# Keeping back the side matmuls of every odd slot of a scan pipeline

## The chip, the core and the metric

The kernel runs on one NeuronCore of a Trainium2 chip. The metric is the device time of one execution in microseconds; the median of the runs shown is 17,875.02 us. The core's engines are named as in the profile: PE (TensorE matmul) and PEld (its weight loads), DVE (VectorE), ACT (ScalarE), POOL (GpSimd), and SP (the queue that issues the DMAs). Each of them executes its own instructions in the order in which the program issues them; between engines they wait for each other through semaphores.

## The reference

Eight images of 48 x 48 x 96 go through four residual layers, `x = x + f(norm(x))`, all in float32:

- layer 0 and layer 3 are 2-D selective scans: an input projection to 192 channels and a 3 x 3 depthwise convolution, then a scan with 16 states per channel over four directions (rows and columns, each forward and backward), then a layer norm, a gate and an output projection;
- layer 1 upsamples by two in the frequency domain, applies a two-layer network with a quadratic in between, filters and downsamples;
- layer 2 scans each row and each column by itself, forward and backward, with a short causal convolution, a gate and an output projection.

The heart of layers 0, 2 and 3 is the same recurrence, with one state for each of 192 channels x 16:

```python
dA = jnp.exp(dl[..., None] * A)
h = h * dA + (dl * u)[..., None] * Bv[:, :, None, :]
y = jnp.einsum('bkdn,bkn->bkd', h, Cv)
```

## The kernel before

**Three stages.** `ss2d("l0", ...)` computes layer 0, `lines(...)` layer 2, and `ss2d("l3", ...)` layer 3. Layer 1 has no stage of its own. It is a *guest* (`class Guest`): a generator of small pieces, each a few matmuls into one PSUM bank and an ACT operation that reads the bank. The guest's pieces are slipped into layers 0 and 2.

**Blocks, turns and slots.** In each stage `scans` walks over 160 blocks (8 images x 4 directions x 5 blocks of up to 480 pixels). A block has four *turns* (`q` = 0 to 3), so a stage has 640 turns and the kernel 1,920. A turn handles two of a block's eight *slots*, `at = 2 * t` and `at + 1`, so slot 2q is even and slot 2q + 1 is odd. On the engines, one turn consists of:

- DVE: three scans (`scan(t, 0..2)`, L304) and those products `dbu` (L272) that are not on POOL. The scans read the decay factors from PSUM, where there are two buffers `ps_da`.
- ACT: three pairs of exponentials that fill those buffers (`make_da`, L296). The first pair of the next turn, `make_da(t + 1, 0)`, is issued after the first side step of this turn. ACT also copies rows to PSUM (`copy_b`, L253).
- POOL: two products with C (`make_hc`, L310), one for each half-turn, and its share of the `dbu` products (L272).
- PE: two *sums over states*, `reduce(t - 1, 0)` and `reduce(t - 1, 1)` (L330 and L332), each four matmuls on quarters of the array. They belong to the turn before and each needs one `make_hc`. Where a new half block begins (`slot == 0` in `reduce`, which falls into the turns with odd `q`) an *opening* matmul (L326) is issued ahead of the first sum. There is one PSUM bank `ps_y`: the opening waits until the finished sum of the half block before has been copied out (`ysum`, ACT L716, in `ss2d`; `gated`, DVE L876, in `lines`).

**Side work.** After the second sum comes `aside(at)`, and at the end of the turn `aside(at + 1)`. A side step settles the guest piece of the slot before (its ACT operation), issues the loads of the slot, takes one step of `side` (convolution, norm, output of an image), runs the steps that `stage1` has planned for this slot, and lets the guest issue its next pieces. Most of it is written so that a matmul is issued in one slot and its reader, on ACT or DVE, in the next one or two. In `ss2d`, for example, the step of slot 3 issues a matmul `raw(0)` (L665), slot 4 reads it (`biased(0)`, ACT L669) and issues `raw(1)`, slot 5 reads that, and slot 6 takes a softplus (L693). In `lines`, slot 3 is half of the convolution (L813), slot 7 two `dt` matmuls (L841) that need ACT's copy `bcl` (L835) of the same slot, and slot 9 (slot 1 of the next block) the two gate matmuls (L854), which ACT reads in slot 10 (`zb`, L863); the projection (L885) follows in that slot and is added by DVE a slot later (L893, L891). Guest pieces are read by ACT at L1073, L1102, L1109, L1119, L1125 and L1165. In layer 0 a guest piece can be issued in slots 2 to 6; in `lines` in slots 0, 2, 3 and 6.

The order of one turn is written out by hand:

```python
            if t > 0:
                reduce(t - 1, 0)
            scan(t, 1)
            make_da(t, 2)
            copy_b(at + 3)
            make_dbu(at + 3, nc.vector)
            if t > 0:
                reduce(t - 1, 1)
            aside(at)
            begin(t + 2)
            make_hc(t, 0)
            make_da(t + 1, 0)
            scan(t, 2)
            copy_b(at + 4)
            finish(at + 1)
            aside(at + 1)
```

On PE the queue therefore reads, turn after turn: first sum, second sum, matmuls of the even slot, matmuls of the odd slot.

## Time and profile before

| what | value |
|---|---|
| runs shown | 17,866.05 / 17,875.02 / 17,882.01 us |
| profiled execution | 17,892.97 us, span 17,891.2 us, mean granted PE clock 0.777 |
| busy, whole span | PE 82%, DVE 89%, ACT 78%, POOL 85% |
| stage `l0`, its 640 turns | from 115 to 5,965 us |
| stage `lines` | from 6,061 to 12,310 us |
| stage `l3` | from 12,434 to 17,857 us |

The busy shares are averages over three stages that differ in their side work, so a stage has to be read by itself. PE's busy time is modelled from pipelined matmuls, so a busy PE is not a PE at its peak. "PEclk" in the profile is the granted share of PE's full clock. A wait is listed as the idle time of an engine before an instruction, with the instruction that ended it.

### The profile page before, as it was taken

How to read it: one execution, taken by the hardware profiler on the slowest of the kernel's cores; microseconds unless marked ns; L12 is line 12 of the kernel's file. 1: busy time of each engine (PE TensorE's matmuls, PEld its weight loads, DVE VectorE, ACT ScalarE, POOL GpSimd, SP SyncE). 2: the span in 40 equal slices, each digit the busy share in tenths (PEclk: the TensorE clock that was granted, in tenths of full speed). 3: DMA queues.
4: the chain of work that ended last, by engine and by line, in shares of the span. 5: the costliest groups of instructions: out<-in, count | busy, mean ns of one | idle time of the engine just before them, and what ended most of it. 6: DMA issues, size and time to landing. Idle time of an engine off the chain costs nothing. (4 is left out here: it accounts for less than half of the span.)

```text
span 17891.2 us, 168509 instructions
## 1 busy us (share of the span) xinstructions
PE 14657.1 (82%) x53740; PEld 4413.6 (25%) x53740; DVE 15977.6 (89%) x9976; ACT 13880.5 (78%) x20932; POOL 15155.4 (85%) x7999
## 2 busy tenths in 40 slices
PE   6878888878787788888888888987778778778776
PEld 1223232323232322222222222222122222222221
DVE  7998999898888788787888889996999999999998
ACT  6877878878787677787777778786878778778776
POOL 7988888888888677787777778886999999999998
PEclk7778777878786788888888888888677777777776
DMA  4555545454545334443443444443455455455454
GB/s 141 176 166 171 172 165 170 162 178 159 168 159 174 131 137 153 137 150 133 152 144 140 144 146 156 154 154 124 170 173 173 169 174 176 168 176 177 169 175 142
DMA packets 887917, 2843.63 MB, mean 159 GB/s; under 512 B 353468, under 2 KB 421788, under 8 KB 760206
## 3 DMA queue, kind: packets, MB, share of 16 engines
q1 hardware_dynamic: 887022, 2832.85, 46.7%
q8 instruction: 421, 6.90, 0.2%
q14 instruction: 474, 3.88, 0.1%
HBM read 2384.40 MB, written 448.17 MB: 158 GB/s over the span
## 5 line engine op out<-in xcount | busy, mean ns | idle before, releaser
L304 DVE TENSOR_TENSOR_SCAN dbu<-ps_da,dbu 128x968 f32<-128x968 f32 (+3 forms) x5760 | 11823.5, 2074 | 923.6 <-ACT ps_da L296 757.6
L310 POOL TENSOR_TENSOR dbu<-dbu,bc 128x1440 f32<-128x1440 f32 (+1 forms) x3840 | 10071.8, 2635 | 2349.7 <-DVE dbu L304 2264.9
L296 ACT ACTIVATE ps_da<-dd,w_l_a 128x484 f32<-128x484 f32 (+3 forms) x11520 | 7424.3, 649 | 2511.4 <-DVE dbu L304 2282.1
L330 PE MATMUL ps_y<-dbu,w_red 128*32 128x480 f32 (+1 forms) x23040 | 4741.8, 731 | 1238.5 <-POOL dbu L310 1225.2
L332 PE MATMUL ps_y<-dbu,w_red 128*32 128x480 f32 (+1 forms) x7680 | 4705.9, 731 | 0.0
L272 DVE TENSOR_TENSOR dbu<-dd,ps_b 128x962 f32<-128x962 f32 (+5 forms) x2880 | 3828.8, 1329 | 270.3 <-ACT ps_b L253 160.7
L272 POOL TENSOR_TENSOR dbu<-dd,bc 128x481 f32<-128x481 f32 (+5 forms) x2240 | 3914.8, 1763 | 23.3 <-DMA dd<-dd 18.9
L330 PEld LDWEIGHTS ps_y<-dbu,w_red 128*32 128x32 f32 x23040 | 797.7, 126 | 5072.2 <-POOL dbu L310 2976.6
L253 ACT COPY ps_b<-bc 128x482 f32<-128x482 f32 (+3 forms) x2720 | 1448.3, 532 | 209.9 <-DVE dbu L272 164.4
L536 PE MATMUL ps_side<-xpad,w_l_cw 128*128 128x480 f32 (+1 forms) x2880 | 1466.0, 651 | 42.1 <-ACT g_room L1109 12.7
L296 ACT ACT_TABLE_LOAD x993 | 1274.0, 1283 | 17.4
L665 PE MATMUL ps_s<-bcl,dtw 6*96 6x480 f32 (+1 forms) x1280 | 952.0, 835 | 290.6 <-ACT dds L669 133.5
L813 PE MATMUL ps_sb<-xpad,w_l_cw 128*128 128x480 f32 (+1 forms) x1280 | 879.0, 839 | 90.4 <-ACT g_room L1109 33.7
L326 PE MATMUL ps_y<-ysum,w_ident 96*96 96x480 f32 (+1 forms) x960 | 764.5, 887 | 207.5 <-ACT ysum L716 203.3
L470 POOL TENSOR_TENSOR dds<-dds,u 96x960 f32<-96x960 f32 (+1 forms) x320 | 706.8, 2209 | 209.7 <-ACT dds L693 209.3
L675 PE MATMUL ps_s<-u,w_l_xp 96*38 96x480 f32 (+1 forms) x1280 | 837.5, 785 | 53.1 <-ACT g_room L1109 13.6
L813 PE MATMUL ps_sa<-xpad,w_l_cw 128*128 128x480 f32 (+1 forms) x1280 | 864.6, 826 | 0.1
L536 PEld LDWEIGHTS ps_side<-xpad,w_l_cw 128*128 128x128 f32 x2880 | 579.0, 216 | 890.5 <-issue 784.3
L332 PEld LDWEIGHTS ps_y<-dbu,w_red 128*32 128x32 f32 x7680 | 730.8, 126 | 0.0
L716 ACT COPY ysum<-ps_y 96x480 f32<-96x480 f32 (+1 forms) x640 | 472.0, 738 | 62.9 <-PE ps_y L332 61.5
L830 PE MATMUL ps_sa<-ub,w_l_xp 96*38 96x480 f32 (+1 forms) x640 | 344.3, 669 | 205.1 <-ACT ub L820 205.1
L669 ACT ACTIVATE dds<-ps_s,w_l_dtb 96x480 f32<-96x480 f32 (+1 forms) x640 | 405.5, 634 | 132.8 <-DMA dd<-dds 84.1
(236 smaller groups left out, 12311.2 us busy)
## 6 DMA issues: line engine op xcount, KB each, us to landing
dd<-dd SPq DMA_DIRECT2D x512, 1452.0 KB
bc<-bcd SPq DMA_DIRECT2D x1536, 480.0 KB
dd<-dd SPq DMA_DIRECT2D x256, 1440.0 KB
dd<-dds SPq DMA_DIRECT2D x512, 363.0 KB
dd<-dd SPq DMA_DIRECT2D x128, 1164.0 KB
bc<-bcd SPq DMA_DIRECT2D x384, 384.0 KB
dd<-dds SPq DMA_DIRECT2D x256, 360.0 KB
dd<-dd SPq DMA_DIRECT2D x64, 1152.0 KB
```

What stands on the lines that cost most here:

```text
L253: nc.scalar.copy(bps[t][:, :bcs[t][0].shape[1]], bcs[t][0])
L272: engine.tensor_mul(o, du, by.unsqueeze(1).to_broadcast([P, hi - lo, by.shape[1]]))
L296: nc.scalar.activation(da[:, at:at + b.m], b.got[half][:, u % 3, 0, :], AF.Exp, scale=a[:, b.k, ci:ci + 1])
L304: nc.vector.tensor_tensor_scan(db, da, db, 0.0, ALU.mult, ALU.add)
L310: nc.gpsimd.tensor_mul(h, h, bcs.pop(2 * t + sub)[1].unsqueeze(1).to_broadcast([P, 3, n]))
L326: nc.tensor.matmul(ys[b, half][:DH, :n], lhsT=lhsT, rhs=rhs, start=True, stop=False)
L330: nc.tensor.matmul(y[32 * g:32 * g + 32, :n], lhsT=wc["red"][:, :32], rhs=hc[:, g, b.at], start=False, stop=(slot == 3))
L332: nc.tensor.matmul(y[DH:, :n], lhsT=wc["red"][:, 32:], rhs=hc[:, 2, b.at], start=(slot == 0), stop=(slot == 3))
L536: nc.tensor.matmul(pu[:, :n], lhsT=flat[:, at:at + P], rhs=xpad[:, r0 + dy:r0 + dy + nr, dx:dx + W], start=(tap == 0), stop=(tap == 8))
L665: nc.tensor.matmul(got["p"][:DH, :n], lhsT=dtw[2 * NS:, b.k, half, :], rhs=b.bcl[2 * NS:, :n], start=True, stop=True)
L675: nc.tensor.matmul(got["p"][:NBC, :n], lhsT=w[f"{l}_xp"][:, b.k, half, :], rhs=u[:, half], start=(half == 0), stop=(half == 1))
L813: nc.tensor.matmul(got["u", half][:, :n], lhsT=flat[:, at:at + P], rhs=shifted(off), start=(tap == 0), stop=(tap == 3))
```

## The change

All matmuls of side steps are issued through a new function `mm` in place of `nc.tensor.matmul`. While an odd slot's `aside` runs, `mm` only notes the matmul in a list; the list is issued in the next turn, between the first and the second sum. Nothing else of the odd slot moves: its ACT, DVE and POOL operations and its DMA issues stay where they were. Two places are kept out of it by `at_once` (the convolution of the first image's last blocks, and the output of the last image), and the guest gets one more slot of waiting per image before it loads an image into a room that its last matmuls read.

```diff
+    held = []
+
+    def mm(*of, **how):
+
+        if held:
+            held[-1].append((of, how))
+        else:
+            nc.tensor.matmul(*of, **how)
+
+    def at_once(steps):
+
+        while True:
+            kept, held[:] = held[:], []
+            clear = next(steps, steps)
+            held[:] = kept
+            if clear is steps:
+                return
+            yield clear
+
...
+        kept = []
+
+        def give_out():
+            for of, how in kept:
+                nc.tensor.matmul(*of, **how)
+            kept.clear()
+
         for t, (b, q) in enumerate(turns):
...
             if t > 0:
                 reduce(t - 1, 0)
+            give_out()
             scan(t, 1)
             make_da(t, 2)
             copy_b(at + 3)
...
             finish(at + 1)
+            held.append(kept)
             aside(at + 1)
+            held.pop()
             if q == NG // 2 - 1 and b.k == order[-1] and b.last:
+                give_out()
                 for _ in beside:
                     while tail:
                         tail.pop(0)()
+        give_out()
         if guest:
             guest.settle()
...
-                for n, _ in enumerate(conv(0, BLKS[3:])):
+                for n, _ in enumerate(at_once(conv(0, BLKS[3:]))):
...
-                    for m, clear in enumerate(post(job, [blk])):
+                    for m, clear in enumerate(at_once(post(job, [blk]))):
...
                 yield "wait", 2
                 yield slim(last)
+                yield "wait", 1
                 yield "do", lambda: nc.sync.dma_start(x, self.xin[b])
```

The rest of the diff replaces `nc.tensor.matmul` by `mm` in `norm_scale`, `conv`, `post`, both `stage1`, `done` of `lines`, and the guest.

On PE the queue afterwards reads: first sum, matmuls of the odd slot of the turn before, second sum, matmuls of the even slot.

More of the change, by code (lines that the diff above doesn't have):

```diff
@@ L158, in run @@
                 got["p"] = psum()
-                nc.tensor.matmul(got["p"][:C, :1], lhsT=wc["gmat"], rhs=v, start=True, stop=True)
+                mm(got["p"][:C, :1], lhsT=wc["gmat"], rhs=v, start=True, stop=True)
             behind(run)
@@ L535, in conv @@
                             at = (2 * tap + half) * DH
-                            nc.tensor.matmul(pu[:, :n], lhsT=flat[:, at:at + P],
+                            mm(pu[:, :n], lhsT=flat[:, at:at + P],
                                              rhs=xpad[:, r0 + dy:r0 + dy + nr, dx:dx + W],
@@ L543, in gate @@
                                 got["z"] = ps("s1", 1)
-                                nc.tensor.matmul(got["z"][:DH, :n], lhsT=w[f"{l}_in"][:, (2 + half) * DH:(3 + half) * DH],
+                                mm(got["z"][:DH, :n], lhsT=w[f"{l}_in"][:, (2 + half) * DH:(3 + half) * DH],
                                                  rhs=xpad[:C, 1 + r0:1 + r0 + nr, 1:1 + W], start=True, stop=True)
@@ L564, in post @@
                 for half in range(2):
-                    nc.tensor.matmul(pm[:DH, :n], lhsT=mean, rhs=y[:, half, s], start=(half == 0), stop=(half == 1))
+                    mm(pm[:DH, :n], lhsT=mean, rhs=y[:, half, s], start=(half == 0), stop=(half == 1))
                 yield
@@ L576, in post @@
                     for half in range(2):
-                        nc.tensor.matmul(pv[:CH, c:c + 1], lhsT=sq[:, half, c * CH:(c + 1) * CH], rhs=ones,
+                        mm(pv[:CH, c:c + 1], lhsT=sq[:, half, c * CH:(c + 1) * CH], rhs=ones,
                                          start=(half == 0), stop=(half == 1))
@@ L596, in post @@
                     at = r0 * W // CH + c
-                    nc.tensor.matmul(pr[:DH, c * CH:(c + 1) * CH], lhsT=var[:, at:at + 1].to_broadcast([CH, DH]),
+                    mm(pr[:DH, c * CH:(c + 1) * CH], lhsT=var[:, at:at + 1].to_broadcast([CH, DH]),
                                      rhs=wc["ident"], start=True, stop=True)
@@ L606, in post @@
                 for half in range(2):
-                    nc.tensor.matmul(po[:C, :n], lhsT=wnb[:, half, :], rhs=z[:, half, :n], start=(half == 0), stop=False)
+                    mm(po[:C, :n], lhsT=wnb[:, half, :], rhs=z[:, half, :n], start=(half == 0), stop=False)
                 yield
                 for half in range(2):
-                    nc.tensor.matmul(po[:C, :n], lhsT=w[f"{l}_out"][:, half, :], rhs=y[:, half, s],
+                    mm(po[:C, :n], lhsT=w[f"{l}_out"][:, half, :], rhs=y[:, half, s],
                                      start=False, stop=(half == 1))
@@ L664, in raw @@
                 got["p"] = ps("s1", 1)
-                nc.tensor.matmul(got["p"][:DH, :n], lhsT=dtw[2 * NS:, b.k, half, :], rhs=b.bcl[2 * NS:, :n],
+                mm(got["p"][:DH, :n], lhsT=dtw[2 * NS:, b.k, half, :], rhs=b.bcl[2 * NS:, :n],
                                  start=True, stop=True)
@@ L674, in s0 @@
                 for half in range(2):
-                    nc.tensor.matmul(got["p"][:NBC, :n], lhsT=w[f"{l}_xp"][:, b.k, half, :], rhs=u[:, half],
+                    mm(got["p"][:NBC, :n], lhsT=w[f"{l}_xp"][:, b.k, half, :], rhs=u[:, half],
                                      start=(half == 0), stop=(half == 1))
@@ L793, in lines @@
                 p = ps("sa" if half else "sb", 1)
-                nc.tensor.matmul(p[:DH, :C], lhsT=wl["l2_outpt"][:, k, half, :], rhs=wl["l2_out"][:, k, :],
+                mm(p[:DH, :C], lhsT=wl["l2_outpt"][:, k, half, :], rhs=wl["l2_out"][:, k, :],
                                  start=True, stop=True)
@@ L812, in run @@
                         at = ((b.k * 4 + tap) * 2 + half) * DH
-                        nc.tensor.matmul(got["u", half][:, :n], lhsT=flat[:, at:at + P],
+                        mm(got["u", half][:, :n], lhsT=flat[:, at:at + P],
                                          rhs=shifted(off), start=(tap == 0), stop=(tap == 3))
@@ L829, in s3 @@
                 for half in range(2):
-                    nc.tensor.matmul(got["p"][:NBC, :n], lhsT=w["l2_xp"][:, b.k, half, :], rhs=b.ub[:, half, :n],
+                    mm(got["p"][:NBC, :n], lhsT=w["l2_xp"][:, b.k, half, :], rhs=b.ub[:, half, :n],
                                      start=(half == 0), stop=(half == 1))
@@ L840, in s5 @@
                     got[half] = ps("sb" if half else "sa", 1)
-                    nc.tensor.matmul(got[half][:DH, :n], lhsT=dtw[2 * NS:, b.k, half, :], rhs=b.bcl[2 * NS:, :n],
+                    mm(got[half][:DH, :n], lhsT=dtw[2 * NS:, b.k, half, :], rhs=b.bcl[2 * NS:, :n],
                                      start=True, stop=True)
@@ L853, in s7 @@
                     got["z", half] = ps("sb" if half else "sa", 1)
-                    nc.tensor.matmul(got["z", half][:DH, :n], lhsT=w["l2_inz"][:, b.k, half * DH:(half + 1) * DH],
+                    mm(got["z", half][:DH, :n], lhsT=w["l2_inz"][:, b.k, half * DH:(half + 1) * DH],
                                      rhs=shifted(0)[:C], start=True, stop=True)
@@ L884, in project @@
                 for h in range(2):
-                    nc.tensor.matmul(got["o"][:C, :n], lhsT=wo[:, b.k, h, :], rhs=t[:, h, :n], start=(h == 0), stop=(h == 1))
+                    mm(got["o"][:C, :n], lhsT=wo[:, b.k, h, :], rhs=t[:, h, :n], start=(h == 0), stop=(h == 1))
             def add():
@@ L1005, in linear @@
                 for m in range(NM):
-                    nc.tensor.matmul(p[:C, :C], lhsT=w1h[:, m, :], rhs=w2l[:, m, :], start=(m == 0), stop=(m == NM - 1))
+                    mm(p[:C, :C], lhsT=w1h[:, m, :], rhs=w2l[:, m, :], start=(m == 0), stop=(m == NM - 1))
             def constant(p):
                 for m in range(NM):
-                    nc.tensor.matmul(p[:C, :1], lhsT=w2[:, m, :], rhs=c01[:, m:m + 1], start=(m == 0), stop=(m == NM - 1))
+                    mm(p[:C, :1], lhsT=w2[:, m, :], rhs=c01[:, m:m + 1], start=(m == 0), stop=(m == NM - 1))
             yield "do", fetch
@@ L1042, in mean_of @@
                 def mean_of(v):
-                    return lambda p: nc.tensor.matmul(p[:C, :1], lhsT=wc["gmat"], rhs=v, start=True, stop=True)
+                    return lambda p: mm(p[:C, :1], lhsT=wc["gmat"], rhs=v, start=True, stop=True)
                 def deviate():
@@ L1066, in items @@
                 yield "wait", 1
-                yield ("psum", lambda p: nc.tensor.matmul(p[:C, :1], lhsT=wlin, rhs=shift, start=True, stop=True),
+                yield ("psum", lambda p: mm(p[:C, :1], lhsT=wlin, rhs=shift, start=True, stop=True),
                        lambda p: nc.scalar.activation(bl, p[:C, :1], AF.Identity, bias=bias))
                 def heighten(s0):
-                    return ("psum", lambda p: nc.tensor.matmul(p[:UG, :HS * W], lhsT=upt, rhs=xt[:, s0:s0 + HS, :],
+                    return ("psum", lambda p: mm(p[:UG, :HS * W], lhsT=upt, rhs=xt[:, s0:s0 + HS, :],
                                                                start=True, stop=True),
@@ L1099, in run @@
                         for j in range(nh):
-                            nc.tensor.matmul(p[:C, j * UG:(j + 1) * UG], lhsT=up[:, j, :], rhs=upt, start=True, stop=True)
+                            mm(p[:C, j * UG:(j + 1) * UG], lhsT=up[:, j, :], rhs=upt, start=True, stop=True)
                         self.soon.append((1, lambda: load_up(n + 1)))
@@ L1106, in hidden @@
                     cols = bands[n][1] * UG
-                    return ("psum", lambda p: nc.tensor.matmul(p[:, :cols], lhsT=w1[:, m * P:(m + 1) * P], rhs=xu[:, :cols],
+                    return ("psum", lambda p: mm(p[:, :cols], lhsT=w1[:, m * P:(m + 1) * P], rhs=xu[:, :cols],
                                                                start=True, stop=True),
@@ L1116, in run @@
                             for m in range(NM):
-                                nc.tensor.matmul(p[:UG, (j - j0) * C:(j - j0 + 1) * C], lhsT=hq[:, m, j * UG:(j + 1) * UG],
+                                mm(p[:UG, (j - j0) * C:(j - j0 + 1) * C], lhsT=hq[:, m, j * UG:(j + 1) * UG],
                                                  rhs=w2q[:, m, :], start=(m == 0), stop=(m == NM - 1))
@@ L1127, in out @@
                             ydd[:, h0:h0 + nh, :], yd[:, :nh * C].rearrange("p (h c) -> p h c", c=C))))
-                    return "psum", lambda p: nc.tensor.matmul(p[:W, :nh * C], lhsT=downt, rhs=ym[:, :nh * C],
+                    return "psum", lambda p: mm(p[:W, :nh * C], lhsT=downt, rhs=ym[:, :nh * C],
                                                               start=True, stop=True), out
@@ L1159, in run @@
                     def run(p):
-                        nc.tensor.matmul(p[:C, :ZW * H], lhsT=wl, rhs=v, start=True, stop=False)
+                        mm(p[:C, :ZW * H], lhsT=wl, rhs=v, start=True, stop=False)
                         for j in range(ZW):
-                            nc.tensor.matmul(p[:C, j * H:(j + 1) * H], lhsT=zs[n % 2][:, j, :], rhs=downt,
+                            mm(p[:C, j * H:(j + 1) * H], lhsT=zs[n % 2][:, j, :], rhs=downt,
                                              start=False, stop=(j == ZW - 1))
```

## The prediction

> **What bounds the kernel now.** I read the page's busy row first, then the busy time by stage, then the waits of DVE and ACT in stage `l0`, then the timeline of one turn there.

> ```profile
> PE 14657.1 (82%) x53740; PEld 4413.6 (25%) x53740; DVE 15977.6 (89%) x9976; ACT 13880.5 (78%) x20932; POOL 15155.4 (85%) x7999
> ```

> ```profile
> 110.00:5965.00 5855.00, 4806.83 (x19712) 1618.23 (x19710) 5291.89 (x3257) 4631.43 (x7201) 5079.09 (x2840) 0.77 0.51 167
> 6060.00:12310.00 6250.00, 5391.29 (x18221) 1600.30 (x18221) 5419.86 (x3471) 4860.93 (x7097) 4906.15 (x2234) 0.83 0.41 146
> 12434.00:17857.00 5423.00, 4229.64 (x15183) 1101.13 (x15184) 5206.99 (x3170) 4289.51 (x6484) 5070.82 (x2840) 0.72 0.50 171
> ```

> The columns are the stretch, its length, busy PE, PEld, DVE, ACT, POOL, then PEclk, DMA share and GB/s. DVE sets the pace: in `l3` it works 5,207 of 5,423 us and nothing on PE can win more than the other 216. In `l0` it idles 563 us and in `lines` 830 us. A change to PE's order gains or loses only through those idles.

> DVE's and then ACT's waits in `l0` (200 to 5,960 us):

> ```profile
> DVE dbu L304 <- ACT ps_da L296: 329.8, 266, 4.8
> DVE xi L613 <- PE ps_side L610: 44.2, 15, 5.6
> DVE ysum L568 <- PE ps_side L565: 29.3, 10, 4.9
> ```

> ```profile
> ACT ps_da L296 <- DVE dbu L304: 632.4, 559, 6.5
> ACT g_room L1109 <- PE ps_side L1107: 65.0, 53, 6.9
> ACT g_room L1165 <- PE ps_side L1162: 55.2, 22, 6.0
> ACT g_room L1119 <- PE ps_side L1117: 55.0, 34, 4.2
> ```

> DVE waits for ACT's exponentials, and ACT, in front of them, waits for PE's side matmuls. So the question is when a side matmul's reader gets its bank.

> A turn where this is visible (start, length; q = 3 starts at 3639.05):

> ```profile
> 3637.77 5.43 POOL L310 TENSOR_TENSOR dbu<-dbu,bc 128x1440 f32<-128x1440 f32 x2
> 3638.89 0.55 ACT L716 COPY ysum<-ps_y 96x480 f32<-96x480 f32 x1
> 3639.95 2.88 PE L536 MATMUL ps_side<-xpad,w_l_cw 128*128 128x384 f32 x4 [1.67 <-ACT g_room L1125]
> 3642.62 0.94 PE L1107 MATMUL ps_s<-g_room,g_w 96*128 96x219 f32 x2
> 3642.93 0.55 ACT L253 COPY ps_b<-bc 128x482 f32<-128x482 f32 x1
> 3643.35 1.01 PE L326 MATMUL ps_y<-ysum,w_ident 96*96 96x480 f32 x2
> 3643.59 0.45 ACT L1109 ACTIVATE g_room<-ps_s,g_b 128x219 f32<-128x219 f32 x1
> 3644.06 1.28 ACT L693 ACT_TABLE_LOAD   x1
> 3647.67 1.37 ACT L296 ACTIVATE ps_da<-dd,w_l_a 128x484 f32<-128x484 f32 x2
> 3649.07 2.17 DVE L304 TENSOR_TENSOR_SCAN dbu<-ps_da,dbu 128x968 f32<-128x968 f32 x1 [0.61 <-ACT ps_da L296]
> ```

> Slot 5's matmuls (L536, L1107) run first, then the opening L326 and the sums. ACT is free at 3643.48, just as L1107 ends. Behind its reader L1109 stand a table load, the softplus, a second table load and the exponentials, and DVE waits 0.61 us for those. This chain has no slack. In the new order the opening can start at 3639.44 (L716 done) and the first sum when the first of the two products L310 is, near 3640.5 (3637.77 and half of 5.43); it takes 0.8 and the odd work, 3639.95 to 3643.35 now, 3.4: it ends near 3644.7, and L1109 starts some 1.2 us later.

> **How I counted.** Each engine keeps the issue order, so the trace can be counted off against the program: three scans are a turn, the sums' records mark its PE part. I took each turn between where the even slot's matmuls leave PE free and the second sum, and put the pieces in the new order with their traced lengths: opening and first sum start when PE is free and POOL's product and the `ps_y` copy are there; the odd matmuls follow. Below, times are means after the turn's first scan.

> **The change part by part.** No instruction is added on any engine and no DMA moves on SP; the guest's extra slot is 8 turns' halves (about 5 us each), hidden because the guest only has to be ahead of `lines`; uncovered it would be 40 us.

> *Stage `l0`, turn q = 3 with a guest piece of slot 5 (99 turns).* PE is free of even work at 1.0, waits 1.0 for a bank, does 3.5 us of odd work and ends at 5.65; ACT comes free at 5.78. In the new order opening 1.5 and sum 1.06 come first; 1.0 of these 2.56 us fills the former wait, the rest pushes the odd work to about 7.3. The reader starts 1.5 us later on average; slack behind it is 0.2. Turn by turn the delay beyond slack adds to 134 us.

> *Turn q = 2 (157).* `raw(0)` of slot 3 gets behind the first sum (1.3 us), which itself waits for POOL; its reader L669 starts 0.47 later against a slack of 1.1 on average. Beyond slack: 38 us. The readers in q = 0 and 1: 13 us. The next late thing is `raw(1)`, which needs the bank of L669: about half of 0.47 us reaches slot 5's piece in 99 turns, 23 us. Stage sum 208. A turn that has grown gives PE time to catch up, so I count three quarters: 156 us.

> *Stage `lines`.* Slot 7's `dt` matmuls now wait for `bcl` while PE stands idle:

> ```profile
> PE ps_sa L841 <- ACT bcl L835: 167.7, 158, 3.1
> ```

> The first sum (1.3 us) fits into this wait, so the second sum comes 1.1 us earlier at q = 0; at q = 2 it (0.8) fits into a mean wait of 0.7 before the convolution. `gated` (DVE waits 232.6 us for it in this stage) gains 33 + 44 us and loses 46 in turns where the first sum waits for POOL and the convolution could have run. At q = 1 the opening waits for `gated` until the turn's end, about 1.2 us, in which the gate matmuls used to run: they end at 5.2 instead of 2.7, ACT's `zb` starts 0.84 later, beyond slack 53 us. The projection, for whose result DVE waits 212.6 us, starts earlier in some turns (-107) and later in others (+57). Sum -77 + 46 + 53 - 50 = -28 us.

> *Stage `l3`.* The bank of `raw(0)` is 3.3 us later but ACT comes for it at 3.6 anyway: 0.54 later, slack 1.35, beyond it 32 us. There is no guest.

> *DVE's own readers in `l0` and `l3`* (L568, L580, L601, L613; 382 of them, which wait 157 us in all now). About half belong to odd slots. Nothing shows their new wait; the least is a gain of all 78 us of their share, the most 1.5 us more for each of 191, 286. Nearest is their own row, 0.41 each now. I take +30, toward the low end: the odd work ends at 4.2 to 5.6 in most turns (7.4 at q = 3 of `l0`), and DVE reaches the even side step only after its second scan and a product, past 6.

> *SP.* A guest load that overwrites what a held matmul reads (L1162's rows) stands on SP in front of the block loads until PE is done, up to one odd segment (3.5 us). These loads land turns ahead; 0 to 80 us for the some 48 such pieces at half of that; I take 0, as L1162's present waits on DMA are 14.4 us in all.

> *Clock.* The groups of a sum start 0.80 us apart at 3031.52 and 0.42 apart at 3042.68, with the stages' clock at 0.72 to 0.83. [...] at the 0.83 of `lines` instead of 0.77, the 6.0 us of opening, sum and odd work would take 0.4 us less, 43 us over the 99 turns. [...] I count 0 and keep 45 us either way.

> Sum: 156 - 28 + 32 + 30 = +190 us on the profiled execution's 17,893 (span 17,891.2 and 1.8 around it), 18,083. It stood 18 us above the median of the runs shown, so **18,065 us**.

> **The rivals.** *Faster: the freed PE waits win.* If all gains in `lines` come (33 + 44 + 107 = 184) without the losses, and `l0`'s delayed readers disappear in turns that DVE bounds (a quarter of 208 left, 52), the time is 132 us lower, about 17,743. It decides as soon as the mean delay at slot 5 stays under some 0.5 us. For it: 830 us of DVE idle in `lines`, and PE waits of 168 us there that the first sum covers exactly. Against it: the reader chain of q = 3 ends in a DVE wait.

> *No change: everything is absorbed.* ACT has 20% idle; if delays and gains cancel (208 shrinks to 60, `lines` gives 60), 17,875. Against it: the slack of q = 3 is 0.2 us.

> *Much slower: the delays reach DVE in full and multiply.* With no slack behind them the readers' delays are 26 + 29 + 74 + 147 = 276 us in `l0` (q = 0 to 3), 142 in `lines` and 85 in `l3`; DVE's own readers at a third of their bound add 95. Less 100 of the gains in `lines` that is +498, or 18,373. It needs banks that are given back late to stall the even matmuls too.

> **How the numbers follow.** This kernel's measurement can tell about 0.2%, 36 us, from no change. The main case has 0.62 (by itself 17,930 to 18,250), the multiplied one 0.13, the faster one 0.15, the absorbed one 0.10, of which 0.04 falls on faster, 0.05 on same and 0.01 on slower. That makes faster 0.19, same 0.05, slower 0.76. The range takes in most of the outer cases and the clock's 45: 17,760 to 18,380.

> **What would show it.** Right: in `l0` ACT's waits for guest banks (L1109, L1119, L1165, L1102, L1125) together grow by 100 us or more, L669's wait for L665 grows from 37 us to over 100 in all stages, and DVE's wait for L296 in `l0` grows from 330 us; in `lines` the wait of L841 for L835 nearly vanishes while that of L326 for `gated` grows; the second sum's wait for POOL shrinks. The stage `l0` takes over 100 us longer, `lines` changes by less than 100, `l3` by about 30. Wrong: `lines` shorter by 150 us, or `l0` no longer than before.

## The result and the profile after

The changed kernel takes 18,099.53 us (median of four runs, 18,096.96 to 18,132.6) against 17,878.51 for the kernel before on the same chip: a ratio of 1.0129, 95% interval 1.0111 to 1.0146, or 221 us more. The profiled execution is the longest of the four, 18,132.6 us, so the profile shows 240 us of growth where the medians show 221.

In the code of this kernel every line lies further down: the scan is L323 (was L304), the exponentials L315 (L296), POOL's product L329 (L310), the sums L349 and L351 (L330, L332), the opening L345 (L326), `ysum` L747, `gated` L907, the readers of guest pieces L1104, L1133, L1140, L1150, L1156 and L1197 (L1073, L1102, L1109, L1119, L1125, L1165), `biased` L700 (L669). A side matmul that is issued at once has line L138, one that was kept back L417. So the lines alone tell which kind of matmul a reader waited for.

The page's busy row:

```profile
PE 15119.0 (83%) x53740; PEld 4307.7 (24%) x53740; DVE 15988.2 (88%) x9976; ACT 13887.6 (77%) x20933; POOL 15152.2 (84%) x7999
```

DVE, ACT and POOL have the same work to within 11 us each; all of their growth is idle time. By stage (`l0`, `lines`, `l3`; columns as before: stretch, length, busy PE, PEld, DVE, ACT, POOL, PEclk, DMA share, GB/s):

```profile
115.00:6091.00 5976.00, 5013.52 (x19647) 1586.67 (x19648) 5299.36 (x3256) 4622.97 (x7191) 5078.47 (x2840) 0.75 0.50 163
6185.00:12484.00 6299.00, 5525.68 (x18270) 1558.76 (x18270) 5415.26 (x3470) 4870.34 (x7104) 4904.13 (x2234) 0.83 0.41 144
12608.00:18095.00 5487.00, 4342.85 (x15180) 1064.69 (x15181) 5212.37 (x3169) 4290.79 (x6481) 5069.39 (x2840) 0.71 0.49 169
```

Taken from the first scan of a stage to the first scan of its last turn, `l0` grows by 125.7 us, `lines` by 49.9, `l3` by 65.0. The granted clock of `l0` fell from 0.77 to 0.75, and that of `l3` from 0.72 to 0.71. Counted in the same way over all the traces of this document, a stage in which nothing is kept back lasts 5,836 to 5,859 us in `l0` (seven traces), 6,231 to 6,249 in `lines` (four) and 5,416 to 5,423 in `l3` (eight). Differences of some 15 us between two traces of `l0` or `lines` can therefore be chance. In three other traces in which all of `lines` is kept back it lasts 6,276 to 6,280 us, so 27 to 31 over before: the 49.9 of this longest run are on the high side.

DVE's waits in `l0` (us in total, times, longest):

```profile
DVE dbu L323 <- ACT ps_da L315: 422.5, 268, 6.0
DVE xi L644 <- PE ps_side L138: 37.5, 13, 5.8
DVE ysum L599 <- PE ps_side L138: 22.8, 10, 5.2
```

The scan's wait for the exponentials grew by 93 us. The other two rows are DVE's own readers of side matmuls; with their smaller rows, for matmuls that were kept back among them, the four readers wait 99 us for PE instead of 95. ACT's waits there:

```profile
ACT ps_da L315 <- DVE dbu L323: 590.6, 528, 6.5
ACT dds L700 <- PE ps_s L417: 60.6, 33, 4.4
ACT g_room L1150 <- PE ps_s L417: 57.8, 26, 6.1
ACT g_room L1150 <- PE ps_side L417: 54.8, 24, 4.2
ACT g_room L1140 <- PE ps_s L417: 51.8, 27, 3.8
```

The four rows that end in L417 are waits for matmuls that were kept back. The five readers of guest pieces that the prediction named wait 469.7 us for PE in `l0`, all rows together, against 322.5 before.

The turn that the prediction showed, counted off to the same place (it starts at 3718.74):

```profile
3718.84 0.55 ACT L747 COPY ysum<-ps_y 96x480 f32<-96x480 f32 x1
3719.44 1.92 PE L345 MATMUL ps_y<-ysum,w_ident 96*96 96x480 f32 x2 [1.22 <-ACT ysum L747]
3721.29 1.02 PE L349 MATMUL ps_y<-dbu,w_red 128*32 128x480 f32 x3
...
3722.09 1.02 PE L349 MATMUL ps_y<-dbu,w_red 128*32 128x480 f32 x3
...
3722.88 0.54 ACT L272 COPY ps_b<-bc 128x482 f32<-128x482 f32 x1
3723.05 2.70 PE L417 MATMUL ps_side<-xpad,w_l_cw 128*128 128x384 f32 x4
3725.59 0.53 PE L417 MATMUL ps_s<-g_room,g_w 96*128 96x219 f32 x2
3726.16 0.44 ACT L1140 ACTIVATE g_room<-ps_s,g_b 128x219 f32<-128x219 f32 x1 [2.73 <-PE ps_s L417]
3726.62 1.28 ACT L724 ACT_TABLE_LOAD   x1
...
3730.23 1.37 ACT L315 ACTIVATE ps_da<-dd,w_l_a 128x484 f32<-128x484 f32 x2
3731.64 2.17 DVE L323 TENSOR_TENSOR_SCAN dbu<-ps_da,dbu 128x968 f32<-128x968 f32 x1 [3.23 <-ACT ps_da L315]
```

The opening L345 stands at the head of PE's queue and waits for the copy L747. Behind it come the first sum and only then the kept matmuls. ACT waits 2.73 us for the guest's bank where it waited for nothing before; the reader starts 7.42 us into the turn instead of 4.54, and the scan at its end comes 2.88 us later too (12.90 instead of 10.02), with a wait of 3.23 instead of 0.61. Not one of the 2.88 us was absorbed on the way. The turn is a bad one, as the part on the clock shows: over 98 turns of this kind the kept work ends 2.0 us later on average.

### The profile page after: what moved, and what is told of

Same layout as the page of the kernel before. It is cut to its first block, busy times and chain, and to the rows that moved or that the text cites. A ratio compares the mean times of both kernels' runs of the same rounds, so it can differ in the third digit from the quotient of the medians.

```text
span 18130.8 us, 168513 instructions
## 1 busy us (share of the span) xinstructions
PE 15119.0 (83%) x53740; PEld 4307.7 (24%) x53740; DVE 15988.2 (88%) x9976; ACT 13887.6 (77%) x20933; POOL 15152.2 (84%) x7999
## 5 line engine op out<-in xcount | busy, mean ns | idle before, releaser
L323 DVE TENSOR_TENSOR_SCAN dbu<-ps_da,dbu 128x968 f32<-128x968 f32 (+3 forms) x5760 | 11830.5, 2075 | 1130.6 <-ACT ps_da L315 940.8
L329 POOL TENSOR_TENSOR dbu<-dbu,bc 128x1440 f32<-128x1440 f32 (+1 forms) x3840 | 10064.9, 2632 | 2511.5 <-DVE dbu L323 2437.6
L315 ACT ACTIVATE ps_da<-dd,w_l_a 128x484 f32<-128x484 f32 (+3 forms) x11520 | 7423.9, 649 | 2484.5 <-DVE dbu L323 2251.3
L349 PE MATMUL ps_y<-dbu,w_red 128*32 128x480 f32 (+1 forms) x23040 | 4972.8, 737 | 1340.7 <-POOL dbu L329 1329.2
L351 PE MATMUL ps_y<-dbu,w_red 128*32 128x480 f32 (+1 forms) x7680 | 4924.3, 737 | 0.0
L349 PEld LDWEIGHTS ps_y<-dbu,w_red 128*32 128x32 f32 x23040 | 675.7, 122 | 5049.6 <-POOL dbu L329 3212.8
L345 PE MATMUL ps_y<-ysum,w_ident 96*96 96x480 f32 (+1 forms) x960 | 803.0, 929 | 398.8 <-ACT ysum L747 393.2
L417 PE MATMUL ps_s<-u,w_l_xp 96*38 96x480 f32 x1256 | 819.4, 783 | 69.7 <-ACT g_room L1140 34.0
L417 PE MATMUL ps_sb<-xpad,w_l_cw 128*128 128x480 f32 (+1 forms) x1264 | 866.0, 836 | 7.2 <-ACT g_room L1140 3.7
L138 PE MATMUL ps_sa<-xpad,w_l_cw 128*128 128x480 f32 (+1 forms) x1280 | 864.6, 826 | 1.3 <-ACT g_room L1104 1.3
L138 PE MATMUL ps_side<-xpad,w_l_cw 128*128 128x480 f32 (+1 forms) x1760 | 786.0, 582 | 4.7 <-issue 3.0
L138 PE MATMUL ps_s<-bcl,dtw 6*96 6x480 f32 (+1 forms) x648 | 550.9, 948 | 149.9 <-ACT dds L700 146.9
L345 PE MATMUL ps_y<-ub,diag 96*96 96x480 f32 (+1 forms) x640 | 434.4, 770 | 225.6 <-DVE gated L907 225.2
L351 PEld LDWEIGHTS ps_y<-dbu,w_red 128*32 128x32 f32 x7680 | 621.4, 122 | 0.0
L417 PE MATMUL ps_side<-xpad,w_l_cw 128*128 128x480 f32 (+1 forms) x1120 | 607.9, 671 | 0.0
L700 ACT ACTIVATE dds<-ps_s,w_l_dtb 96x480 f32<-96x480 f32 (+1 forms) x640 | 405.9, 634 | 247.8 <-PE ps_s L417 150.5
L138 PE MATMUL ps_sa<-ub,w_l_xp 96*38 96x480 f32 (+1 forms) x640 | 360.8, 697 | 205.8 <-ACT ub L851 205.8
```

The costliest lines, as they stand in the source:

```text
L138: nc.tensor.matmul(*of, **how)
L315: nc.scalar.activation(da[:, at:at + b.m], b.got[half][:, u % 3, 0, :], AF.Exp, scale=a[:, b.k, ci:ci + 1])
L323: nc.vector.tensor_tensor_scan(db, da, db, 0.0, ALU.mult, ALU.add)
L329: nc.gpsimd.tensor_mul(h, h, bcs.pop(2 * t + sub)[1].unsqueeze(1).to_broadcast([P, 3, n]))
L345: nc.tensor.matmul(ys[b, half][:DH, :n], lhsT=lhsT, rhs=rhs, start=True, stop=False)
L349: nc.tensor.matmul(y[32 * g:32 * g + 32, :n], lhsT=wc["red"][:, :32], rhs=hc[:, g, b.at], start=False, stop=(slot == 3))
```

## Experiments

**Which stage.** The theory to be tested was the prediction's: a kept matmul's reader comes later, and where no slack stands behind the reader, DVE's next scan does. In the expectations it is theory A. Its rivals: the clock falls because PE's gaps are rearranged (B); the guest's extra slot and its loads pay (C). In the later expectations B is any matmul that is kept back, by its PE time, D is `raw(0)` of slot 3, and E is A with `lines` divided by whether the guest still works. Three kernels keep matmuls back in one stage only (`hold_l3` and `hold_lines` alike, with the tuple in their own stage):

```diff
-            held.append(kept)
+            if (at + 1) % NG in keep:
+                held.append(kept)
             aside(at + 1)
-            held.pop()
+            held.clear()
...
-        scans(..., conv(0, BLKS[1:3]), guest)
+        scans(..., conv(0, BLKS[1:3]), guest, (1, 3, 5, 7) if l == "l0" else ())
```

> Odd slots are kept back in stage l0 only. Theory A (readers of held matmuls stand behind the opening and the first sum): +110 to +160 us on before, nearly all of it in the turns q = 3 and q = 2 of l0; the other stages as before. Rival B (the new order runs PE at a lower clock, and everything on PE takes longer): the loss of about 221 us spreads over the stages as PE's busy time does, so about 73 us here. Rival C (the PE order is harmless, the extra slot of the guest and loads that stand behind held matmuls on SP cost): most of the 221 us here and in lines together, and none in l3.

> Odd slots are kept back in stage lines only. Theory A: gains and losses nearly cancel, -30 to +60 us on before; the second sum of q = 0 about 1 us earlier, the gate matmuls of slot 9 over 2 us later. Rival B: about 82 us, by PE's busy share. Rival C: 50 to 110 us.

> Odd slots are kept back in stage l3 only, where no guest runs. Theory A: +30 to +80 us on before, in q = 1 and q = 2 (ACT's L669 waiting for raw(0), DVE's own readers). Rival B: about 65 us. Rival C: 0.

| kernel | median us | ratio to before (95%) | us over before | mean clock |
|---|---|---|---|---|
| `hold_l0` | 18,008.76 | 1.0066 (1.0053 to 1.0079) | 123 | 0.772 |
| `hold_lines` | 17,935.32 | 1.0028 (1.0018 to 1.0039) | 50 | 0.777 |
| `hold_l3` | 17,952.09 | 1.0036 (1.0023 to 1.0048) | 67 | 0.775 |

Each stage pays by itself, and the three nearly add up (240 against 221). `lines` loses 50 us, and the granted clock is not what it loses by: in the changed kernel, where this stage takes 49.9 us more, its clock is 0.83 as before; `hold_l3`'s 67 us would also fit the 65 of the clock's rival.

**Which reader in `l0`.** The first kernel is the changed one with a guest piece of slot 5 issued at once; all else is kept back:

```diff
+                own, held[:] = held[:], [] if slot == 5 else held[:]
                 self.put(self.psum(banks.pop(0)), *of)
+                held[:] = own
```

> As the changed kernel, but the guest's matmuls of slot 5 (only l0 has them) are issued at once, ahead of the opening, while the convolution taps of slot 5 stay kept back. Theory A: the turn q = 3 of l0 goes back from 12.06 towards 11.5 us, 160 blocks: 60 to 100 us less than the changed kernel, 18,000 to 18,040. Rival B: the order of the bulk of PE's work is unchanged, within 20 us of the changed kernel. Rival C: within 20 us as well, since the guest keeps its extra slot and most loads stand where they stood.

It takes 18,017.64 us, 1.008 (1.0066 to 1.0094): by the medians 82 us less than the changed kernel. In its stage `l0` DVE waits

```profile
DVE dbu L323 <- ACT ps_da L315: 321.8, 276, 4.9
```

which is the 329.8 of before again, not 422.5. A mean turn with q = 3, from first scan to first scan, lasts 11.49 us before, 12.04 after and 11.14 here, while those with q = 0 and 1 get 0.2 and 0.1 us longer. The stage ends 28 us above the kernel before, where the changed kernel has 126. So one kind of matmul, in the turns where it occurs, makes most of what `l0` lost.

**Which slots.** Two kernels keep back the matmuls of half of the odd slots, in all stages (`(1, 5)` or `(3, 7)` for `keep`):

> Only slots 1 and 5 are kept back, in all stages: those that come behind an opening (L326) as well as the first sum. Theory A (opening and first sum ahead of the held matmuls): most of the loss, +140 to +190 us on before: about 90 in l0 (slot 5's guest piece), 40 to 60 in lines (gate matmuls of slot 9), 20 to 40 in l3. Rival B (any held matmul costs, by its PE time): half, about 110 us. Rival D (raw(0) of slot 3 with its chain of readers is what costs): under 60 us.

> Only slots 3 and 7 are kept back, in all stages: those that come behind the first sum alone. Theory A: +30 to +80 us on before, nearly all from raw(0) in the q = 2 turns of l0 and l3; lines within 20 us of before. Rival B: about 110 us. Rival D: 160 us or more. With slots_1_5 it should add up to the changed kernel's 220 to 240 us if the two don't act on each other.

`slots_1_5` takes 18,048.4 us, 1.009 (1.0076 to 1.0103), with a mean clock of 0.780; `slots_3_7` takes 17,962.69 us, 1.0043 (1.003 to 1.0055), with 0.767. The one that loses twice as much time has the higher clock: the clock doesn't order these kernels. By stage, `slots_1_5` adds 128 us in `l0`, 6 in `lines` and 14 in `l3`; `slots_3_7` adds 44 in `lines` and in `l3`, and its 15 less in `l0` are within what traces of that stage differ by. The totals, 166 and 81 us, are about as theory A had them, the stages are not: it had `lines` pay 40 to 60 for slots 1 and 5 and less than 20 for 3 and 7.

**`raw(0)` of slot 3.** The changed kernel with this one matmul issued at once:

```diff
                 got["p"] = ps("s1", 1)
-                mm(got["p"][:DH, :n], lhsT=dtw[2 * NS:, b.k, half, :], rhs=b.bcl[2 * NS:, :n],
+                nc.tensor.matmul(got["p"][:DH, :n], lhsT=dtw[2 * NS:, b.k, half, :], rhs=b.bcl[2 * NS:, :n],
```

> As the changed kernel, but raw(0) of slot 3 in l0 and l3 (L665 of the kernel before) is issued at once. Theory A: the q = 2 turns of l0 and l3 lose their 0.19 and 0.14 us, so 30 to 60 us less than the changed kernel. Rival D: over 120 us less. Rival B: under 15 us less, one matmul of some twenty.

It takes 18,085.45 us, 1.0114 (1.01 to 1.0128). That is 14 us less than the changed kernel by the medians and 27 by the ratios, neither clear of noise and less than the 30 to 60 of theory A. The small sum hides two different stages. `l3` gets 48 of its 65 us back: ACT's wait there, 8.0 us before, is in the changed kernel and then in this one

```profile
ACT dds L700 <- PE ps_s L417: 89.9, 58, 4.4
```

```profile
ACT dds L700 <- PE ps_s L696: 8.7, 12, 0.9
```

(L696 is `raw(0)`, issued directly.) `l0`, which has the same step, does not get shorter (5,986 us against 5,976): there ACT's readers of guest pieces, still kept back, wait 161 instead of 110 us in the turns with q = 2, which go from 8.17 to 8.49 us in the mean, while those with q = 3 go from 12.04 to 11.77.

**What is wrong in `lines`.** The prediction had `lines` a little shorter. By its account slots 3 and 7 hold the gains (the convolution and the `dt` matmuls) and slot 1 the loss (the gate), so slots 3 and 7 alone, in `lines` alone, had to be about even:

> Slots 3 and 7 are kept back in lines only; the gate matmuls of slot 9 (slot 1) stay where they were, and l0 and l3 are as before. Theory A: what hold_lines lost (50 us) came from the gate matmuls, ACT's L863 behind them (80 us more waiting) and the projection's add (L893, 30 us more); so -25 to +15 us on before. If the second sum that comes 1 us earlier at q = 0 is worth what the prediction said (gated 33 us), -30 or better; if the exponentials of the next turn end last there anyway, no gain, about 0. Rival B: about two thirds of hold_lines, +30 to +35 us.

It takes 17,948.78 us, 1.0035 (1.0022 to 1.0047), or 67 us more, outside the -25 to +15 that this account gave. So slots 3 and 7 are not even, whatever the gate matmuls do.

Counting off `hold_lines` by image then showed two regimes. While the guest works (images 0 to 4), PE is behind and turns last some 10 us; afterwards (images 6 and 7) they last some 9 us, and image 5 lies between. Four kernels separate these. `keep` becomes a function of the slot; `none` keeps nothing back and has only the guest's extra slot, and `mix` came from the readings of the others:

```diff
+  none:         lambda slot: False
+  lines_guest:  lambda slot: slot % 2 and guest.made < nb      (in lines; else nothing)
+  lines_later:  lambda slot: slot % 2 and guest.made == nb     (in lines; else nothing)
+  mix:          lambda slot: slot in (1, 3) and guest.made < nb   (in lines)
+                lambda slot: slot == 7                            (in l0; l3 nothing)
```

> Nothing is kept back; only the guest's extra slot per image is left of the change. Theory A: it moves the guest's pieces by one slot and costs nothing, within 25 us of before (lines looked 10 to 19 us shorter where only another stage was kept back). Rival C (the guest's extra slot and its loads cost): +50 us or more.

> In lines the odd slots are kept back only while the guest still works (images 0 to 4 and part of 5); l0 and l3 as in none. Theory E (with the guest PE is behind, the held gate matmuls wait for ACT's banks anyway, and the first sum fills that wait; the second sum, the projection and DVE's add come earlier): 25 to 55 us less than none. Theory A as written before the first run (the gate matmuls lose in every turn of q = 1): 20 to 40 us more than none.

> The counterpart: in lines the odd slots are kept back only after the guest has finished. Theory E: without the guest PE is early, the opening waits for gated and the gate matmuls with it; L863 and the add L893 come later: 65 to 100 us more than none, and with lines_guest it adds up to hold_lines (about 50 us). Theory A as written: 10 to 20 us more.

> Only what seemed to gain: slots 1 and 3 of lines while the guest works, and slot 7 of l0. Theory E: 40 to 110 us less than none, 17,775 to 17,845: q = 1 of lines shorter by about 0.6 us and q = 2 by 0.2 over some 100 blocks, l0 shorter by 15 to 40. If the gains of the traces were noise or don't add, within 25 us of none.

| kernel | median us | ratio to before (95%) | us over `none` |
|---|---|---|---|
| `none` | 17,878.45 | 1.0001 (0.9993 to 1.0009) | |
| `lines_guest` | 17,843.53 | 0.998 (0.9973 to 0.9987) | -35 |
| `lines_later` | 17,973.26 | 1.005 (1.0037 to 1.0062) | 95 |
| `mix` | 17,796.75 | 0.9953 (0.994 to 0.9967) | -82 |

The guest's extra slot costs nothing. The same edit gains 35 us while PE is behind and loses 95 when it is ahead. In the second regime PE and DVE wait, first `none`, then `lines_later` (the last 1,439 and 1,512 us of the stage):

```profile
PE ps_y L345 <- DVE gated L909: 14.0, 13, 4.1
```

```profile
DVE x L926 <- PE ps_sa L138: 8.6, 10, 1.2
```

```profile
PE ps_y L345 <- DVE gated L909: 149.4, 45, 5.5
```

```profile
DVE x L926 <- PE ps_sa L138: 65.3, 25, 4.3
DVE dbu L323 <- ACT ps_da L315: 61.2, 64, 2.8
DVE gated L909 <- PE ps_y L351: 34.0, 19, 3.4
```

The opening L345 waits for `gated`, which comes at the end of DVE's turn. An early PE used to fill this time with the gate matmuls; now they stand behind it. What follows them, ACT's `zb` and the projection, comes late, and DVE waits 56.7 us more for the projection at L926; its two other rows are 6 and 12 us above those of `none`. A mean turn with q = 1 goes from 8.75 to 10.24 us. The trace of `slots_1_5` shows that the gate is enough for this: in `lines`, where slot 5 issues no matmul, it keeps back the gate's alone, and is 59 us shorter than `none` in images 0 to 4 and 73 longer in images 5 to 7. So the gate matmuls lose time in the one regime and nearly win it back in the other.

In the first regime PE reaches the opening when `gated` is mostly done. DVE's waits there, in `none` and in `lines_guest`:

```profile
DVE dbu L323 <- ACT ps_da L315: 238.7, 220, 3.3
DVE gated L909 <- PE ps_y L351: 182.6, 85, 5.6
DVE x L926 <- PE ps_sa L138: 158.8, 60, 4.7
```

```profile
DVE dbu L323 <- ACT ps_da L315: 275.8, 252, 3.3
DVE gated L909 <- PE ps_y L351: 144.1, 59, 5.5
DVE x L926 <- PE ps_sa L138: 117.0, 57, 3.8
```

`gated` and the projection each gain about 40 us, and the exponentials take back 37.

`mix` keeps back only slots 1 and 3 in this regime and slot 7 in `l0`. It beats both kernels. By its trace it gains 71 us in `lines`, where that of `lines_guest` gains 36; its 14 us in `l0` are no more than traces of that stage differ by. The two differ in `lines` by slot 7 alone, so slot 7 costs about 35 us while the guest works. The traces show what it costs there: the two `dt` matmuls keep their banks until ACT's softplus (L881) has read them, and the next matmul that goes to such a bank waits for it, in `lines_guest` and then in `mix`

```profile
PE ps_sa L138 <- ACT dds L881: 140.0, 62, 17.9
```

```profile
PE ps_sa L138 <- ACT dds L881: 38.6, 25, 15.7
```

The wait for `bcl` that the change was to fill (110 us in `mix`, 17 in `lines_guest`) is paid again here by the matmuls behind. No run takes this wait alone away.

## Why the prediction was right in sign and close in size

The forecast of 18,065 us lies 34 us under the median, and its main case happened: readers without slack in `l0`. But its terms were off by more than their sum: 190 us were predicted and 240.6 are in the profile. That the sum came so close is in part luck: `l0` was counted 35 us too large and `lines` 78 too small.

| term | predicted us | measured us |
|---|---|---|
| `l0` | 156 | 125.7 |
| `lines` | -28 | 49.9 |
| `l3` | 32 | 65.0 |
| DVE's own readers | 30 | in the stages: 5 in `l0`, 31 in `l3` |

*Slot 5 in `l0`: right in place, too large in size.* The guest's readers in the turns q = 3 wait 115 us more (177 to 292), and the first scans of the turns behind them 92 us more for ACT (124 to 216). `guest5_at_once` takes these back to 69. The absence of slack was read rightly from the timeline. But the turns q = 3 grew by 88 us in all. For them 134 + 23 us were counted, or 118 after the three quarters.

*Slot 3 in `l0`: about right in size, its cause not separated.* ACT's waits before `biased` in the turns q = 2 grew by 42 us and these turns by 30, where 38 were counted (28 after the three quarters). But `raw0_at_once` gives none of it back in `l0`.

*`l3`: right, with both of its terms.* DVE's wait for the exponentials grew from 82.7 to 109.3 us, where 32 were counted for `raw(0)`, and the waits of DVE's own readers from 61 to 93. `raw0_at_once` returns 48 of the 65 us, as both waits shrink there, to 88 and 74 us. The 30 us for the own readers, taken for `l0` and `l3` together with nothing to show their new wait, came as 36, nearly all of it in `l3`. That this guess was close is luck.

*`lines`: the step that failed is the projection.* The others can be read from DVE's waits over the stage, whose rows of after are

```profile
DVE dbu L323 <- ACT ps_da L315: 394.9, 365, 3.3
DVE x L924 <- PE ps_sa L138: 207.6, 93, 4.3
DVE gated L907 <- PE ps_y L351: 204.6, 90, 5.5
```

against 331.8, 179.1 and 232.6 before. `gated` gains 28 us (33 + 44 - 46, so 31, were predicted). The exponentials lose 63, where 53 were predicted through `zb`. `zb` itself waits 80 us for held matmuls:

```profile
ACT zb L894 <- PE ps_sb L417: 72.3, 88, 1.3
ACT zb L894 <- PE ps_sa L417: 7.0, 28, 1.1
```

None waited for that before. The projection, counted with -107 + 57 = -50, lost 28 at L924; the smaller add (L891 before) gained 3. The wait at L924 fell by 54 us in images 0 to 4 and rose by 82 after them. So by regime the gain came to half of what was counted, and the loss to more: with no guest PE is early and stands before the opening, and what is behind it, the projection last, comes late by more than the count had.

*Signs.* Of the signs named, those on ACT and DVE came, and of the stages' only `l3`'s "about 30" did not. In `lines` the wait of L841 for `bcl` fell from 167.7 to 20.8 us, and that of the opening for `gated` rose from 33.1 to 221.0:

```profile
PE ps_y L345 <- DVE gated L907: 221.0, 92, 8.6
PE ps_sa L417 <- ACT bcl L866: 20.8, 37, 1.5
```

The second sum's wait for POOL shrank, in `l0` from 275 to 131 us and in `l3` from 603 to 256, as expected. But it only changed its place: the first sum, which was hidden behind the odd matmuls before, now waits for POOL 308 instead of 75 us in `l0` and 537 instead of 192 in `l3`. The two together stay the same in `l3`, and PE's whole wait of this kind rose from 1,225.2 to 1,329.2 us. So the filled gap opened again one step earlier, with work behind it that ACT was waiting for. In `l0` the opening's own wait for `ysum` adds to it, with 74.9 us before and now

```profile
PE ps_y L349 <- POOL dbu L329: 423.0, 320, 7.2
PE ps_y L345 <- ACT ysum L747: 212.3, 154, 4.6
```

*The clock.* Counting 0 was an estimate, and over the 98 turns counted below it held. In the turn shown the clock matters: the granted clock is 0.50 during the opening and the first sum, where it was 0.96 and more before. The opening takes 1.92 us instead of 1.01, and the sum's two halves start 0.80 us apart; in the same turn of the kernel before, at a granted clock of 1.00, they start 0.42 apart:

```profile
3644.30 0.60 PE L330 MATMUL ps_y<-dbu,w_red 128*32 128x480 f32 x3
3644.72 0.58 PE L330 MATMUL ps_y<-dbu,w_red 128*32 128x480 f32 x3
```

Opening and sum are 1.8 us longer together, the odd work 0.3 shorter. That is most of the difference between the 2.88 us here and the 1.2 that were predicted for it. But the turn is not the rule. Over the 98 turns with q = 3 and a guest piece of slot 5, opening, first sum and odd work take 6.02 us together, and 6.00 in `none`, which has the same guest schedule: opening and sum are slower (1.69 and 1.56 us instead of 1.55 and 1.26), the odd work is faster (2.91 instead of 3.42). The odd work ends at 7.60 us instead of 5.57, near the predicted 7.3 and 5.65. The prediction estimated 43 us less for these turns if `l0` ran at the 0.83 of `lines`; instead the clock of `l0` fell by 0.02, from 0.77 to 0.75. No run holds the clock fixed. But at nearly the same clock in `l0`, 0.761 and 0.765, `slots_1_5` loses 128 us there and `slots_3_7` none, and the changed kernel loses 126 at 0.747: most of the loss doesn't come from the clock.

*SP and the guest's extra slot* were counted with 0, and `none` confirms the latter. The guest's loads behind held matmuls were not tried by themselves, but nothing waits longer for them: all engines' waits that a DMA ended fell, in `l0` from 126 to 106 us, in `lines` from 57 to 51 and in `l3` from 134 to 56.

What stays open: whether the late bank of slot 7 is all of what that slot costs in `lines`, which of slot 3's matmuls costs the time in `l0`, and why the three stages by themselves lose 19 us more than together, within the spread of the medians' intervals.

## What to carry to other kernels

A matmul that is moved later in PE's in-order queue is worth what its reader's slack allows, and its new place is priced by what can wait in front of it (here, in `l0`, an opening that waited 212 us for its bank to be copied out, and sums that waited 423 us for POOL), not only by how long that work takes. Work out the slack by regime, where PE is ahead and where it is behind, since the sum over both hid a gain of 35 us and a loss of 95. Ask also what needs the moved matmul's bank next. A gap that is filled on an engine whose input comes from elsewhere can open again in front of the next instruction that needs the same input, as the wait for POOL did here in `l0` (second sum 275 to 131 us, first sum 75 to 308), so a gain at one wait has to be capped by the next wait that ends there.

## What the hardware showed beyond the forecast

The granted PE clock didn't follow the kernel's time: `slots_1_5` had 0.780 at 18,048 us and `slots_3_7` 0.767 at 17,963 us. In `l0` it fell from 0.77 to 0.75 while PE's busy time rose from 4,807 to 5,014 us; the opening above took 1.92 us at a granted clock of 0.50 and 1.01 at 0.96, and the stage issues the same matmuls (19,712 records before, 19,647 after), so this rise is not more load.

| PE busy in a step | next step full, if this one is full | next step full, if this one is at 0.5 |
|---|---|---|
| under 45% | 5 of 637 | 0 of 343 |
| 55 to 65% | 216 of 398 | 0 of 247 |
| 75 to 85% | 462 of 603 | 15 of 395 |
| 95% and more | 2,806 of 2,866 | 1,346 of 2,723 |

So in these traces the full clock was lost after steps in which PE was well at work: 182 of the 398 full steps that were 55 to 65% busy had a step at 0.5 behind them. And of the 2,723 steps at 0.5 with PE busy for 95% or more, 1,346 had a full one behind them, about every second.
